# Gathering one chunk of every tenth or sixth group by single rows: the range of groups is widened

## The chip, the cores and the metric

The kernel runs on one core of one Trainium2 chip. The metric is the device time of one execution in microseconds; before the change it is 5949.51 us, the median of three runs (5947.85, 5949.51 and 5975.21 us). The profile is that of a separate execution.

## The reference

A graph layer in two rounds over 12,500 nodes of 128 features and 200,000 edges. The edges are sorted by their destination `dst`. Cut to what matters:

```python
h = jnp.maximum(_layernorm(x, axis=-1), 0.0)
# node_features = h
w = edge_weight / jnp.maximum(wsum, EPS)[dst]            # wsum, deg: sums over the edges of a node
feat = relu(h @ W_pool + b_pool)
msg = feat[src] * w[:, None]
neigh = segment_max(msg, dst, num_segments=N)            # layer 1
rst = h @ W1_self + neigh @ W1_neigh + b1
h1 = relu(rst / max(norm(rst), EPS))
msg2 = h1[src] * w[:, None]
neigh2 = segment_sum(msg2, dst, num_segments=N) / max(deg, 1)   # layer 2
out = relu(h1 @ W2_self + neigh2 @ W2_neigh + b2)
return x + out
```

What matters here are `feat[src]` and `h1[src]`: for each edge one row of 128 floats (512 bytes) is fetched from a table in device memory, at an address that only the data tell.

## The kernel before

**Tiling.** The edges go in groups of 512 (`G`), 391 of them (`NG`); the last, group 390, has 320 edges. A group has four chunks of 128 edges (group 390 has two whole chunks and one of 64). A chunk becomes a tile of 128 partitions (edges) by 128 floats.

**Stages.** A preparation normalizes the nodes, computes the table `feat_d` and stores it to device memory. It also builds the transposed edge tables (`srcT`, `ewT` and others). The first 14 groups (`FIRST`) are treated from `x` itself, so that they can be fetched before `feat_d` is done. Then comes layer 1, whose loop counter `i` is called a turn: turn `i` fetches group `i` and scales its rows (ACT, L868), transposes them (PE, L869), scans for the running maximum along the edges (DVE, L877) in turn `i + 1`, and selects and adds up the last edge of each node in the turns up to `i + 4`. Finished blocks of 128 nodes go through two matmuls and a norm (`nodes1`) and are stored to the second table, `h_d` (L758, L761). Layer 2 has the same 391 turns with less work in each: DVE builds a selection matrix (L965, L967), PE multiplies it with the fetched rows in turn `i + 1` (L985), DVE adds the result to a window (L994), and `nodes2` stores the output (L781). Layer 2 reads `h_d`, so its first gather waits until all of `h_d` is stored.

**Order.** The order of the instructions on each engine is written out by hand: what is emitted first in a turn stands first in its engine's queue. An engine runs its queue in order, so an instruction that waits holds up what is behind it. SP is the queue of most loads and stores: the weights' rows of the first groups (`gs`, L521), the two-group tiles that mark where a node begins (`kt`, L527), the stores of `h_d`, the index loads (`ri`, L672), and in layer 2 `xr` (L770) and `out` (L781).

**Two ways to fetch a chunk.** The usual one is an indirect DMA issued by GpSimd (POOL), one for each chunk (L446): it takes 128 indices from `srcT` and fetches 128 rows. The fetched groups stand in a ring of buffers. Up to group 63 the ring has 16 slots (some lent by tables that are not needed yet), later 8; a gather waits until its slot has been read.

The second way is the class `Rows`. In every tenth group of layer 1 (`every` 10) and every sixth of layer 2 (`every` 6), the first chunk is fetched by 128 single DMAs of 512 bytes, issued on the hardware queues of SP and ACT: 96 on SP in pieces of 16 and 32 on ACT in pieces of 4 in layer 1, 64 and 64 in pieces of 16 in layer 2. For such a group the 128 indices are loaded into one partition (`ri`, L672), DVE shifts them to byte offsets (L675), the issuing engine loads a piece's offsets into registers (L685) and issues its rows (L689) into the tile `ga`, of which there are three. The pieces are spread over the turns from `g - every - 1` on. The reader waits for all 128 rows (L703): ACT in layer 1, PE in layer 2. `takes` (L658) says which groups are fetched in this way: those that are divisible by `every` and lie between `first` and `end`. L836 and L951 make the two objects.

Of the kernel before, what the change touches and what calls it, by code (L numbers as in the profile page):

```python
# [39 lines left out]
def gnn_kernel(ctx, tc, x, src, dst, ew, w_pool, b_pool, w1s, w1n, b1, w2s, w2n, b2, out):  # L40
# [13 lines left out]
    nc = tc.nc  # L54
# [6 lines left out]
    NG = GF + 1  # L61
# [7 lines left out]
    feat_d = dram.tile([NP, D], F32, name="feat_d")  # L69
    h_d = dram.tile([NP, D], F32, name="h_d")  # L70
# [22 lines left out]
    wk = prep.enter_context(tc.tile_pool(name="n0", bufs=2))  # L93
# [23 lines left out]
    def buffer(g, wide):  # L117
        return ring[g % (WIDE if wide and g < LESS else RING)]
# [317 lines left out]
    def edges_of(g):  # L436

        ne = G if g < GF else TAIL
        return *divmod(g, P), ne, [(j, min(P, ne - j * P)) for j in range(-(-ne // P))]

    def gather(gt, table_d, g, byrow=None, only=None):
        t, r, ne, chunks = edges_of(g)
        for j, k in chunks if only is None else chunks[only:only + 1]:
            if j == 0 and byrow and byrow.takes(g):
                continue
            nc.gpsimd.indirect_dma_start(  # L446
                out=gt[:k, j, :], out_offset=None, in_=table_d[:, :],
                in_offset=bass.IndirectOffsetOnAxis(ap=srcT[:k, t, j, r:r + 1], axis=0))
        return gt
# [257 lines left out]
    def turns(behind):  # L707

        out = {}
        g = i = 0  # L710
        for n in range(HI):
            while g < NG - 1 and (g + 1 - LAG) * RHO < (n + 1) * P:
                g += 1
            i = max(i + 1, g + behind)
            out[i] = n
        return out
# [3 lines left out]
    def window_at(engine, g):  # L720

        if g % BL == 0:
            _, held[engine] = nc.values_load_multi_w_load_instructions(
                bases[0:1, g:min(g + BL, NG)], [engine], min_val=0, max_val=N - 1,
                skip_runtime_bounds_check_because="destinations of edges are nodes, as the gathers have it")
        return held[engine][g % BL]
# [11 lines left out]
    def linear_own(po, t, self_w):  # L738
        nc.tensor.matmul(po, hT[:, t, :], W[self_w], start=True, stop=False)  # L739
# [27 lines left out]
    def x_rows(wk, t, bufs):  # L767
        (q, p, view), = rows_of(x, t, 1)
        xr = wk.tile([P, D], F32, name="xr", bufs=bufs)
        nc.sync.dma_start(xr[:p, :], view[:, 0, :])  # L770
        return xr

    def nodes2(wk, ps, t, nT, xr):

        po = linear(ps, t, nT, "2s", "2n")
        yield
        (q, p, view), = rows_of(out, t, 1)
        o = wk.tile([P, D], F32)
        nc.vector.tensor_tensor(o[:p, :], po[:p, :], b2_all[:p, :], OP.add)
        nc.vector.scalar_tensor_tensor(o[:p, :], o[:p, :], 0.0, xr[:p, :], op0=OP.max, op1=OP.add)  # L780
        nc.sync.dma_start(view[:, 0, :], o[:p, :])  # L781

    def stages(steps):
        for _ in steps:
            pass


    with tc.manual_schedule(), tc.tile_pool(name="ew", bufs=3) as wk, \
# [44 lines left out]

        keep_rows(2, keep_tile())
        carry = NEG
        byrow = Rows(wk, feat_d, 10, [(nc.sync, 96, 16), (nc.scalar, 32, 4)], 30, NG - 16)  # L836
        for i in range(max(turn) + 6):
            if i >= NG:
                window_copy(i - 5)
# [107 lines left out]
    with tc.manual_schedule(), tc.tile_pool(name="ew2", bufs=3) as wk, \  # L947
            tc.tile_pool(name="ep2", bufs=3, space=PSUM) as ps:
        iota = ps.tile([P, LW], F32, bufs=1)
        nc.vector.tensor_copy(iota, cols[:, 0, :])  # L950
        byrow = Rows(wk, h_d, 6, [(nc.sync, 64, 16), (nc.scalar, 64, 16)], 6, NG - 4)  # L951
        nc.vector.memset(agg, 0.0)
        ss, pas, xrs = ({} for _ in range(3))
        turn = turns(3)
        late = None
        for i in range(max(turn) + 2):
            byrow.turn(i)
            byrow.rows(i, nc.sync)
            byrow.rows(i, nc.scalar)
            if i < NG:  # L960
                gts[i] = gather(buffer(i, False), h_d, i, byrow)
                t, r, ne, chunks = edges_of(i)
                ss[i] = wk.tile([P, Q, LW], F32, name="s")
                hit = ps.tile([P, Q, LW], F32, name="hit", bufs=1)
                nc.vector.tensor_tensor(hit, iota[:, None, :].to_broadcast([P, Q, LW]),  # L965
                                        locT[:, t, :, r:r + 1].to_broadcast([P, Q, LW]), OP.is_equal)
                nc.vector.tensor_tensor(ss[i], hit, w2T[:, t, :, r:r + 1].to_broadcast([P, Q, LW]),  # L967
                                        OP.mult)
            if i + 4 in turn:
                xrs[turn[i + 4]] = x_rows(wk, turn[i + 4], 6)  # L970
            if late is not None:
                stages(late)
                late = None
            if i in turn:
                n = turn[i]
                late = nodes2(wk, ps, n, agg[:, n * P:(n + 1) * P], xrs.pop(n))
                next(late)
            g = i - 1
            if 0 <= g < NG:
                chunks = edges_of(g)[3]  # L980
                pas[g] = ps.tile([P, LW], F32, name="pa")
                gt, s = gts.pop(g), ss.pop(g)
                for j, k in chunks:
                    rows_j = byrow.tile(g, nc.tensor) if j == 0 and byrow.takes(g) else gt[:k, j, :]
                    nc.tensor.matmul(pas[g], rows_j, s[:k, j, :], start=j == 0,  # L985
                                     stop=j == len(chunks) - 1)
            if i == NG - 1:
                for n in (HI - 2, HI - 1):
                    own[n] = ps.tile([P, D], F32, name="pn")
                    linear_own(own[n], n, "2s")  # L990
            g = i - 2
            if 0 <= g < NG:
                at = window_at(mybir.EngineType.DVE, g)
                nc.vector.tensor_tensor(agg[:, bass.ds(at, LW)], pas.pop(g), agg[:, bass.ds(at, LW)], OP.add)  # L994
        assert late is None
# [98 lines left out]
def build(inputs):  # L1094
    import numpy as np
    import concourse.bacc as bacc

    nc = bacc.Bacc("TRN2", target_bir_lowering=False, num_devices=1)
    arrays, args = {}, []
    for name in _INS:  # L1100
        a = np.ascontiguousarray(inputs[name])
        arrays[f"in_{name}"] = a
        args.append(nc.dram_tensor(f"in_{name}", a.shape, mybir.dt.from_np(a.dtype),
                                   kind="ExternalInput").ap())
    args.append(nc.dram_tensor("out", inputs["x"].shape, F32, kind="ExternalOutput").ap())
    with tile.TileContext(nc) as tc:
        gnn_kernel(tc, *args)
    return nc, arrays
# [7 lines left out]
```

## Time and profile before

| | |
|---|---|
| median of three runs | 5949.51 us |
| the profiled execution, its own time | 3844.75 us |
| span of the profile, first to last instruction | 3843.0 us |
| POOL busy | 2873.2 us (75%) |
| PE busy, granted clock 0.522 on average | 2317.6 us (60%) |
| DVE busy | 1712.7 us (45%) |
| ACT busy | 882.9 us (23%) |
| gathers from `feat_d` and from `h_d` (L446) | 1472 and 1499 |
| rows by single DMAs, layer 1: SP, ACT | 3360, 1120 |
| rows by single DMAs, layer 2: SP, ACT | 4096, 4096 |
| one row on SP or ACT (L689): issue, register move | 0.228 us, 0.029 us |
| one load of 16 registers on SP (L685) | 1.228 us |
| layer 1's last gather, layer 2's first gather, start | 1940.32 us, 1957.88 us |

The profiled execution is much shorter than the unprofiled runs, by 2104.8 us; nothing in the profile says where those have their additional time. All durations below come from the profiled execution.

The engines' names: PE is TensorE, DVE VectorE, ACT ScalarE, POOL GpSimd and SP SyncE; a name with a q (SPq, ACTq) is that engine's instruction queue, where DMAs are issued. In a line of the profile, `L446` is the line of the kernel, then come the engine, the operation, the tile written, the tiles read, and how often it occurs. "idle before" is the time for which the engine stood still ahead of it, with what ended that.

### The profile page before, as it was taken

To read this page: it belongs to the slowest core of one execution; us is meant where nothing else is said; L and a number is where in the kernel's file an instruction comes from. 1 tells how busy PE (TensorE), PEld (TensorE's weight loads), DVE (VectorE), ACT (ScalarE), POOL (GpSimd) and SP (SyncE) were. 2 spreads that over 40 slices of the span, in tenths; PEclk is the share of its full clock that TensorE was granted. 3 is DMA by queue.
4 is the path that set the end of the run, shared out by engine and by line. 5 is a ranking of instruction groups with operands and counts; after the bars stand their busy time and mean duration, and the time that the engine had idled before them with its cause. 6 is when DMAs were issued, how large, how long until landed. Compare 5 with 4: busy or idle time off the path is not lost.

```text
span 3843.0 us, 61269 instructions
## 1 busy us (share of the span) xinstructions
PE 2317.6 (60%) x8402; PEld 1790.5 (47%) x8402; DVE 1712.7 (45%) x4882; ACT 882.9 (23%) x2996; POOL 2873.2 (75%) x3061
## 2 busy tenths in 40 slices
PE   7666566666666666666655555555555555555555
PEld 5455454444444444444444444444444444444444
DVE  8877666666666666555542222222222222222221
ACT  7644444444444444444410000000000000000000
POOL 6777777777777777777767777777777777777776
PEclk9655555555555555555555555555555555555555
DMA  7433333323333333333312222222222222222222
GB/s 204 122 91 90 87 89 89 89 83 84 86 86 86 86 86 85 85 85 85 84 52 63 62 64 62 62 63 63 63 63 63 62 63 63 63 63 63 63 63 57
DMA packets 224215, 299.55 MB, mean 78 GB/s; under 512 B 70418, under 2 KB 147444, under 8 KB 223798
## 3 DMA queue, kind: packets, MB, share of 16 engines
q0 software_dynamic: 96864, 198.51, 19.8%
q1 hardware_dynamic: 115766, 93.43, 8.5%
q10 hardware_dynamic: 11168, 3.61, 0.6%
q14 instruction: 345, 2.83, 0.2%
q8 instruction: 72, 1.18, 0.1%
HBM read 275.50 MB, written 19.77 MB: 77 GB/s over the span
## 4 chain that ended last, share of the span: by engine, by line
DMA 55%; issue 11%; POOL 8%; PE 7%; DVE 6%; SPq 5%; ACT 4%; ACTq 3%; POOLq 0%; DVEq 0%
DMA gt<-h_d,srcT 33%; DMA gt<-feat_d,srcT 20%; POOL gt L446 8%; PE pa L985 3%; SPq L689 3%; ACTq L689 2%; ACT gs L868 2%; DVE pm L877 2%; PE pm L869 1%; SPq L685 1%; PE pn L739 1%; ACTq L685 1%; PE pn L735 1%; DVE sc L886 1%; DVE sel L897 1%
## 5 line engine op out<-in xcount | busy, mean ns | idle before, releaser
L446 POOL DMA_INDIRECT gt<-h_d,srcT x1499 | 1415.3, 944 | 474.1 <-issue 217.6
L446 POOL DMA_INDIRECT gt<-feat_d,srcT x1371 | 1295.2, 945 | 418.3 <-DMA gt<-feat_d,srcT 165.4
L985 PE MATMUL pa<-s,gt 128*128 128x48 f32 x2998 | 962.3, 425 | 809.2 <-DMA gt<-h_d,srcT 730.4
L985 PEld LDWEIGHTS pa<-s,gt 128*128 128x128 f32 x2998 | 749.7, 312 | 1024.3 <-DMA gt<-h_d,srcT 812.3
L869 PE MATMUL pm<-ident,gs 128*128 128x128 f32 x1507 | 573.0, 463 | 640.2 <-ACT gs L868 557.3
L877 DVE TENSOR_TENSOR_SCAN pm<-kt,carry,pm 128x512 f32<-128x512 bf16 x389 | 499.7, 1285 | 480.7 <-PE pm L869 473.7
L869 PEld LDWEIGHTS pm<-ident,gs 128*128 128x128 f32 x1507 | 284.0, 193 | 877.4 <-ACT gs L868 742.6
L994 DVE TENSOR_TENSOR agg<-pa,agg 128x48 f32 x391 | 81.2, 208 | 1351.6 <-PE pa L985 950.2
L868 ACT ACTIVATE gs<-gt,ewT 128x128 f32<-128x128 f32 x1371 | 489.6, 395 | 584.9 <-DMA gt<-feat_d,srcT 433.6
L926 PEld LDWEIGHTS pa<-sel,rows 128*128 128x128 f32 x1556 | 365.8, 324 | 51.7 <-ACT agg L819 51.3
L926 PE MATMUL pa<-sel,rows 128*128 128x48 f32 x1556 | 369.1, 385 | 17.1 <-ACT agg L819 16.4
L914 PE MATMUL pr<-ident,sc 128*128 128x128 f32 x782 | 243.7, 414 | 0.0
L897 DVE TENSOR_SCALAR sel<-cols,lastT,invT 128x48 f32<-128x48 f32 x782 | 211.0, 323 | 0.0
L886 DVE COPY_PREDICATED sc<-kt,pm 128x256 f32<-128x256 int16 x389 | 172.0, 442 | 13.2
L914 PEld LDWEIGHTS pr<-ident,sc 128*128 128x128 f32 x782 | 168.8, 225 | 0.1
L885 DVE COPY sc<-pm 128x256 f32<-128x256 f32 x391 | 162.0, 414 | 0.0
L967 DVE TENSOR_TENSOR s<-hit,w2T 128x192 f32<-128x192 f32 x391 | 139.8, 357 | 13.5
L904 ACT ACTIVATE rows<-pr 128x256 f32<-128x256 f32 x392 | 142.6, 364 | 0.5 <-PE pr L914 0.5
L965 DVE TENSOR_TENSOR hit<-iota,locT 128x192 f32<-128x192 f32 x391 | 140.4, 359 | 1.1
L819 ACT ACTIVATE agg<-pa 128x48 f32 x389 | 79.0, 203 | 180.5 <-PE pn L735 175.9
L675 DVE TENSOR_SCALAR ri<-ri 1x128 int32<-1x128 int32 x99 | 25.3, 256 | 196.9 <-DMA ri<-in_src 195.8
L739 PE MATMUL pn<-w_2s,hT 128*128 128x128 f32 x196 | 74.2, 483 | 0.0
(228 smaller groups left out, 1685.4 us busy)
## 6 DMA issues: line engine op xcount, KB each, us to landing
ga<-h_d SPq DMA_DIRECT2D x4096, 0.5 KB
ga<-h_d ACTq DMA_DIRECT2D x4096, 0.5 KB
ga<-feat_d SPq DMA_DIRECT2D x3360, 0.5 KB
kt<-keep_d SPq DMA_DIRECT2D x194, 256.0 KB
gt<-h_d,srcT POOLq DMA_INDIRECT x1499
gt<-feat_d,srcT POOLq DMA_INDIRECT x1371
ga<-feat_d ACTq DMA_DIRECT2D x1120, 0.5 KB
h_d<-h SPq DMA_DIRECT2D x98, 64.0 KB
```

The costliest lines, as they stand in the source:

```text
L446: nc.gpsimd.indirect_dma_start(out=gt[:k, j, :], out_offset=None, in_=table_d[:, :], in_offset=bass.IndirectOffsetOnAxis(ap=srcT[:k, t, j, ...
L689: row = eng.dma_start(ga[r + k:r + k + 1, :], self.bytes[None, bass.ds(at[k], 4 * D)])
L868: nc.scalar.activation(gs[:k, j, :], rows_j, AF.Copy, scale=ewT[:k, t, j, r:r + 1])
L869: nc.tensor.transpose(pms[i][:, j * P:j * P + k], gs[:k, j, :], ident[:k, :k])
L877: nc.vector.tensor_tensor_scan(pm[:, :ne], kt[:, :ne], pm[:, :ne], carry, op0=OP.add, op1=OP.max)
L885: nc.vector.tensor_copy(sc[:, :ne // 2], two[:, :, 1])
L886: nc.vector.copy_predicated(sc[:, :ne // 2], new[:, :, 1], two[:, :, 0])
L897: nc.vector.tensor_scalar(sels[g][:k, j, :], cols[:k, 1, :], lastT[:k, t, j, r:r + 1], invT[:k, t, j, r:r + 1], op0=OP.is_equal, op1=OP.mult)
L904: nc.scalar.activation(rws[g][:k, j, :], pr[:k, j, :], AF.Copy)
L914: nc.tensor.transpose(prs[g][:k, j, :], sc[:, j * P:j * P + k], ident)
L926: nc.tensor.matmul(pas[g], rows[:k, j, :], sel[:k, j, :], start=j == 0, stop=j == len(chunks) - 1)
L985: nc.tensor.matmul(pas[g], rows_j, s[:k, j, :], start=j == 0, stop=j == len(chunks) - 1)
```

## The change

Two numbers for each of the two `Rows` objects say where the row fetches begin and end. In layer 1 they began at group 30 and ended ahead of group 375 (`NG - 16`); now they begin at group 20 and end ahead of group 391 (`NG`). In layer 2 they ended ahead of group 387 (`NG - 4`); now they end ahead of group 391. Groups 20, 380 and 390 of layer 1 and group 390 of layer 2 are so fetched with three gathers (two in group 390) and 128 rows, where before it was one gather more and no rows.

```diff
-        byrow = Rows(wk, feat_d, 10, [(nc.sync, 96, 16), (nc.scalar, 32, 4)], 30, NG - 16)
+        byrow = Rows(wk, feat_d, 10, [(nc.sync, 96, 16), (nc.scalar, 32, 4)], 20, NG)
...
-        byrow = Rows(wk, h_d, 6, [(nc.sync, 64, 16), (nc.scalar, 64, 16)], 6, NG - 4)
+        byrow = Rows(wk, h_d, 6, [(nc.sync, 64, 16), (nc.scalar, 64, 16)], 6, NG)
```

The arguments are the pool, the table, `every`, the shares of the queues (queue, rows, rows in a piece), `first` and `end`. What `Rows` does with the last two, with the plan of the pieces:

```python
for g in range(first, end, every):
    begin = g - every - 1
    at = 0
    for eng, n, rb in share:
        for s in range(n // rb):
            turn = max(begin + s * every // (n // rb), 0)
            self.plan.setdefault(turn, []).append((g, eng, at, rb))
            at += rb
...
def takes(self, g):
    return g % self.every == 0 and self.first <= g < self.end
```

For group 20 of layer 1 the pieces on SP go out in turns 9, 10, 12, 14, 15 and 17, for group 390 in turns 379 to 387; for group 390 of layer 2 in turns 383, 384, 386 and 387.

## The prediction

> **What bounds the kernel now.** First the page's busy table with its costliest groups. GpSimd (POOL) is the busiest engine, and nearly all of that is one line, the indirect gather L446:
>
> ```profile
> PE 2317.6 (60%) x8402; PEld 1790.5 (47%) x8402; DVE 1712.7 (45%) x4882; ACT 882.9 (23%) x2996; POOL 2873.2 (75%) x3061
> ...
> L446 POOL DMA_INDIRECT gt<-h_d,srcT x1499 | 1415.3, 944 | 474.1 <-issue 217.6
> L446 POOL DMA_INDIRECT gt<-feat_d,srcT x1371 | 1295.2, 945 | 418.3 <-DMA gt<-feat_d,srcT 165.4
> ```
>
> 944 ns busy and, in the idle column, about 0.3 us before each. So the second view is POOL's list of waits (total us, times, longest us). If another engine held POOL up, a long wait would stand here:
>
> ```profile
> POOL gt L446 <- issue: 375.1, 1235, 0.5
> POOL gt L446 <- DMA gt<-feat_d,srcT: 165.4, 542, 0.3
> POOL gt L446 <- PE pa L985: 119.7, 392, 0.3
> ...
> POOL gt L446 <- DMA ri<-in_src: 16.6, 1, 16.6
> ```
>
> No wait of a gather is above 0.5 us but one, the passage from layer 1 to layer 2. The other releasers only name what finished last before a gap that is always there. The busy-by-stretch view gives the pace: 1321 instructions in 200-1850 us and 1458 in 1960-3780 us, so 1.249 and 1.248 us per gather. POOL's timeline at the passage (start, length, idle before):
>
> ```profile
> 1939.08 0.94 POOL L446 DMA_INDIRECT gt<-feat_d,srcT  x1 [0.30 <-issue]
> 1940.32 0.90 POOL L446 DMA_INDIRECT gt<-feat_d,srcT  x1 [0.30 <-issue]
> 1957.88 0.95 POOL L446 DMA_INDIRECT gt<-h_d,srcT  x1 [16.65 <-DMA ri<-in_src]
> ```
>
> The last gather of layer 1 feeds group 390; ACT takes it at 1942.67, the last nodes drain through PE, ACT and DVE, h is stored, and the next gather starts at 1957.88. The span is thus two rows of gathers at 1.249 us with a drain after each. The chain of waits agrees: it is 33% and 20% landing gathers, and 8% POOL.
>
> Third, SP's timeline, because the change gives SP work. Rows of layer 2:
>
> ```profile
> 3001.78 0.23 SPq L672 DMA_DIRECT2D ri<-in_src  x1
> 3003.41 5.11 SPq L689 DMA_DIRECT2D ga<-h_d  x16
> 3008.62 0.37 SPq L781 DMA_DIRECT2D out<-o  x1
> 3010.38 11.57 SPq L689 DMA_DIRECT2D ga<-h_d  x32
> 3022.01 0.36 SPq L770 DMA_DIRECT2D xr<-in_x  x1
> 3023.44 0.37 SPq L781 DMA_DIRECT2D out<-o  x1
> 3025.20 5.58 SPq L689 DMA_DIRECT2D ga<-h_d  x16
> 3030.89 0.23 SPq L672 DMA_DIRECT2D ri<-in_src  x1
> ```
>
> 16 rows take 5.1 us, and the register load before them (L685) 1.23 us: 6.4 us a piece. A layer 2 period (6 groups, 64 rows on SP) is 4 pieces, 25.6 us, plus about 1.6 us of other issues: 27.2 us, against 23 gathers x 1.249 = 28.7 us. A layer 1 period (10 groups, 96 rows) is 6 x 6.4 = 38.4 plus five kt, two or three h_d, one ri and gaps, about 43 us, against 39 x 1.249 = 48.7 us. SP has 5% to spare in layer 2 and 12% in layer 1. How near that is shows in DVE's waits of 200-800 us:
>
> ```profile
> DVE ri L675 <- DMA ri<-in_src: 94.5, 10, 11.2
> ```
>
> There ACT, PE and DVE still lag behind POOL, SP is their bound, and once in ten groups DVE stands 10 us or so for an index load that sits behind rows in SP's queue.
>
> **What the Trainium skill says.** "Perfetto Trace Analysis", section "DMA Instruction — SWDGE (GPSIMD)": the profiled end of a GpSimd DMA is when the last descriptor is made, not when the data has moved. So I price a gather by start-to-start spacing (1.249 us), not by its bar (0.944); the fixed 0.30 gap agrees. "DMA: Bandwidth & Descriptors", section "Issuing engines are not separate DMA queues": DMAs of all engines end on the same 16 DMA engines, and issuing elsewhere saves only the issuer's time. That is what the change trades; the page's queue table (19.8%, 8.5% and 0.6% busy) leaves the DMA engines room. "Runtime: NRT & Kernel Launch", section "The ~15µs preamble/postamble breakdown": profile total and reported time differ by about 6 us, profile longer. Here the profiled execution is 3844.75 us and the median 5949.51 us, 2104.8 us the other way, so that page doesn't explain it.
>
> **The change part by part.** Layer 1: row groups were 30, 40 to 370 (35); now 20 to 390 (38), adding 20, 380 and 390. Layer 2: 6 to 384 (64), now to 390 (65). Group 390 has 320 edges; its first 128 are a full chunk.
>
> Removed: one gather for each of four groups, 4 x 1.249 = 5.0 us of POOL. POOL never waits inside a layer, so all of it is on the path: 3.75 us before the 1957.88 gather, 1.25 us before the end.
>
> Added on SP: 3 x 96 + 64 = 352 rows x (0.228 issue + 0.029 register move) = 90 us, and 22 register loads x 1.228 = 27 us. On ACT: 3 x 32 + 64 = 160 rows, 41 us, with 24 loads x 0.489 and 4 long ones (up to 1.5), 18 us. Four ri loads (0.233) and four DVE shifts (0.217). All of it lies beside POOL's gathers, in periods where SP had only kt, h_d, xr and out. If that cover goes, an added period costs SP's excess over POOL's pace (the third rival).
>
> Moved in layer 1's tail: SP's kt loads and h_d stores of turns 369 to 387 stand behind row pieces, each up to 6.4 us later, as in the periods before. The last piece for 390 goes out in turn 387, three turns (15 us) before use; the final four h_d stores come later. At nothing. In layer 2's tail the last pieces go out in turns 383 to 387, four turns (20 us) before PE uses them; out stores wait for DVE anyhow. At nothing.
>
> Moved at the start: pieces in turns 9, 10, 12, 14, 15 and 17 stand before gs and kt loads. DVE's L889 of turns 9 and 10 ends at 150.0 and 155.6. A gs load is issued two turns (11 us) ahead of need, so 6.4 us behind a piece still fits. ACT's L851 runs at 148.33 with DVE needing it at 149.32: four rows there (1.5 us) can push DVE by up to 1 us in four turns. What hides it: POOL overwrites the slot of raw group 12 at 171.80 and its last reader, the product that L851 waits for at 164.69, ends just before, so 7 us. From 141 us SP needs 6 x 6.4 + 4 = 42 us, to 183; group 30's first piece went out at 184.82. So at most 2 us of lag is carried on, against slot margins of 13.4 us at group 72 (POOL 385.5, slot free 372.1) and 11.4 us at group 78. At nothing; lower bound 0, upper bound 3 us if the margins are half of what I read.
>
> Sum: 3844.75 - 5.0 = 3839.8, bounds -6 to 0. **To the median:** no view shows where the 2104.8 us are. If they are an offset, the gain stays 5.0 (5944.5); if everything is slower by 5949.51/3844.75 = 1.547, it is 7.7 (5941.8). I take the middle, 5943. The three runs of before spread over 27 us, 0.46%, so 0.5% is about what can be told from no change; my gain is 0.11%.
>
> **Rivals.** (1) Forecast: POOL is the bound, 5943. (2) The gathers go but the layer ends don't move: the drain at 1942-1957 is PE-paced, or the carried lag meets the slots at groups 72 to 80, and 3 to 5 us go back. For it: DVE's 11 us standings. Against: ACT takes each of the last gathers as it lands. 5949, at the worst 5955. (3) Slower: SP's row issue is the bound in unprofiled runs. The profile has it 5% and 12% away, and an SP slower by a factor f with POOL unchanged would lengthen all row periods: 35 x (43f - 48.7) + 64 x (27.2f - 28.7) = 2105 gives f = 1.74, which would explain the whole gap. Then each added layer 1 period costs 43 x 1.74 - 49.9 (40 gathers) = 25 us and the layer 2 one 27.2 x 1.74 - 30.0 = 17 us, 92 us together: 6041. It decides from f = 1.06 in layer 2 and 1.13 in layer 1. Against it: in the one execution seen POOL never waits for a row's consumer. (4) A gain over 0.5%: needs 30 us from four gathers, 7 us each; only spread between runs gives it, say 5915.
>
> **How the numbers follow.** Forecast 0.68, (2) 0.14, (3) 0.12, (4) 0.06. The first two lie within 0.5%: same 0.82, slower 0.12, faster 0.06. The range holds the first two with the spread of the runs, 5920 to 5968, and leaves 0.18 out.
>
> **What would show it.** In the changed kernel's profile: 1469 gathers of feat_d (1371 + 54 + 23 + 12 + 12 before, by buffer) and 1498 of h_d, pace still 1.249 us, no wait of POOL above 0.5 but the passage; the passage's gather near 1954.1, the span near 3838. Wrong if POOL shows waits of several us near 385 us (lag), if the passage's wait grows beyond 16.65 (drain or h_d late), or if the median moves by tens of us while the profiled span moves by 5: then rival (3).

## The result, and the profile after

| | before | after |
|---|---|---|
| median, on one chip | 5957.73 us (6 runs, 5947.85 to 5975.21) | 6011.47 us (6 runs, 5996.57 to 6031.12) |
| ratio, with its 95% interval | | 1.0085 [1.0069, 1.0101] |
| a profiled execution of it, span | 5930.5 us | 6005.4 us |
| gathers of `feat_d` and `h_d` in it | 1472, 1499 | 1469, 1498 |

The change makes the kernel slower by 0.85%, 51 us at before's median (41 to 60 by the interval). The profiled execution of before that the prediction reads (3844.75 us) is like none of the 87 timed executions of that kernel, the shortest of which took 5932.23 us, so its span isn't set against after's; the 5930.5 us are from a second profile of the unchanged kernel.

First the page of after: the busy table, the chain that ended last, and the gathers of `gt` (mean ns of one, then POOL's idle time before them and its main releaser).

```profile
PE 1991.3 (33%) x8402; PEld 1733.3 (29%) x8402; DVE 1683.3 (28%) x4886; ACT 851.6 (14%) x2996; POOL 2867.1 (48%) x3057
...
SPq L689 45%; SPq L685 6%; DVE pm L877 2%; SPq L527 1%; DMA ri<-in_src 1%; SPq L781 1%; DVE sel L897 1%; DVE sc L885 1%; DVE sc L886 1%; SPq L770 0%; SPq L761 0%; PE pf L550 0%; SPq L672 0%; PE pa L985 0%; SPq L150 0%
...
L446 POOL DMA_INDIRECT gt<-h_d,srcT x1498 | 1413.0, 943 | 1620.8 <-PE pa L985 970.3
L446 POOL DMA_INDIRECT gt<-feat_d,srcT x1368 | 1291.1, 944 | 1352.9 <-ACT gs L868 950.4
```

A gather is what it was, 0.943 us busy, but POOL is busy for only 48% of the span: the idle time before these gathers is 2973.7 us, where the first profile has 892.4, some 0.30 us before each. The chain of waits is no longer landing gathers: 45% is SP's row issue and 6% the register loads ahead of it. POOL's list of waits (total us, times, longest us) says for whom it stands:

```profile
POOL gt L446 <- PE pa L985: 970.3, 159, 17.6
POOL gt L446 <- ACT gs L868: 950.4, 175, 42.2
POOL gt L446 <- issue: 730.4, 2303, 2.1
...
POOL gt L446 <- DMA ri<-in_src: 51.5, 1, 51.5
```

In layer 2 it waits for PE and in layer 1 for ACT to read a slot of the ring, up to 17.6 and 42.2 us at a time. What holds these two up stands in the same list, under the other engines:

```profile
DVE ri L675 <- DMA ri<-in_src: 2204.4, 94, 33.7
...
PE pa L985 <- DVE s L967: 1809.9, 88, 47.7
...
DVE pm L877 <- DMA kt<-keep_d: 683.5, 84, 16.4
...
PE pa L985 <- PEq L703: 59.0, 15, 14.0
...
ACT gs L868 <- ACTq L703: 57.6, 16, 12.3
```

It is less the 128 rows themselves (L703) than what stands behind rows in SP's queue. DVE stands for the next index load `ri`, most of it in layer 2, and PE for the selection matrix `s`, which DVE builds only after that; in layer 1 DVE also stands for the `kt` loads, and ACT in turn for work of DVE and PE (266.2 us at L750, 332.6 at L819). In the first profile the three waits of DVE and PE were 195.8, 41.4 and 6.3 us.

SP's timeline in layer 2 of after, as in the prediction's third view (start, length, how many):

```profile
4618.66 0.23 SPq L672 DMA_DIRECT2D ri<-in_src  x1
4620.28 9.12 SPq L689 DMA_DIRECT2D ga<-h_d  x16
4630.11 0.70 SPq L781 DMA_DIRECT2D out<-o  x1
4632.95 22.59 SPq L689 DMA_DIRECT2D ga<-h_d  x32
4655.55 0.35 SPq L770 DMA_DIRECT2D xr<-in_x  x1
4656.00 0.46 SPq L781 DMA_DIRECT2D out<-o  x1
4657.86 5.16 SPq L689 DMA_DIRECT2D ga<-h_d  x16
4663.13 0.23 SPq L672 DMA_DIRECT2D ri<-in_src  x1
```

Between these lines lie register loads (L685), and the same 64 rows take 36.87 us (9.12 + 22.59 + 5.16), where the first profile had 22.26 (5.11 + 11.57 + 5.58). From one index load to the next it is 44.47 us, against 29.1 there. And 16 rows take 9.12 us in one place and 5.16 in another. POOL's timeline beside it (in brackets the idle time before) shows which is which:

```profile
4604.76 0.94 POOL L446 DMA_INDIRECT gt<-h_d,srcT  x1 [0.30 <-issue]
4622.29 0.94 POOL L446 DMA_INDIRECT gt<-h_d,srcT  x1 [16.59 <-PE pa L985]
4623.53 0.94 POOL L446 DMA_INDIRECT gt<-h_d,srcT  x1 [0.30 <-issue]
...
4653.62 0.94 POOL L446 DMA_INDIRECT gt<-h_d,srcT  x1 [0.30 <-issue]
4666.85 0.94 POOL L446 DMA_INDIRECT gt<-h_d,srcT  x1 [12.29 <-PE pa L985]
```

Rows that SP issues while POOL's gathers flow are slow (4623 to 4655); those issued while POOL stands (4657.86 to 4663.02) have the price of the first profile, 0.32 us each with the register move. It is so over the whole trace: from one row's register move to the next row's, SP's rows of layer 2 take 0.87 us on average where gathers start at most 1.3 us before and after, and 0.33 us where POOL has started none for 2.5 us. But gathers alone don't make rows slow: in the first profile all rows go beside gathers that are 1.249 us apart, at 0.33 us.

The stretch ends with the index load that SP issues at 4663.13:

```profile
4664.43 0.22 DVE L675 TENSOR_SCALAR ri<-ri 1x128 int32<-1x128 int32 x1 [26.92 <-DMA ri<-in_src]
4665.49 2.79 PE L985 MATMUL pa<-s,gt 128*128 128x48 f32 x12 [25.55 <-DVE s L967]
```

POOL goes on at 4666.85. So the two hold each other: gathers slow the rows, the loads behind late rows hold DVE, DVE holds PE, PE the slots, and POOL stops until the rows are out.

**Where the 51 us come in.** The next table follows two points through the traces: DVE's scan of a group (L877) in layer 1 and its addition (L994) in layer 2. Each number is how much later after is than the second profile of before, at the same group, in us:

```
layer 1   group  18   +9.4      layer 2   group   0  +53.3
          group  26  +10.5                group  40  +50.4
          group 190  +14.0                group 373  +66.5
          group 365  +26.5                group 375  +62.3
          group 390  +53.0                group 390  +76.7
```

About ten us come at the new rows of group 20, 26.5 between groups 365 and 390 of layer 1, 14.4 between 375 and 390 of layer 2. The rest accumulates over the middle, where the kernels are equal, and single executions differ by as much there.

At layer 1's end the passage shows it. POOL's timeline of after (the last gather of `feat_d` and the first of `h_d`), then SP's:

```profile
2930.08 0.90 POOL L446 DMA_INDIRECT gt<-feat_d,srcT  x1 [0.31 <-issue]
2982.52 0.95 POOL L446 DMA_INDIRECT gt<-h_d,srcT  x1 [51.53 <-DMA ri<-in_src]
```

```profile
2946.30 12.05 SPq L689 DMA_DIRECT2D ga<-feat_d  x32
2958.45 0.36 SPq L527 DMA_DIRECT2D kt<-keep_d  x1
2958.90 0.38 SPq L761 DMA_DIRECT2D h_d<-h  x1
2960.68 5.15 SPq L689 DMA_DIRECT2D ga<-feat_d  x16
2965.93 0.35 SPq L527 DMA_DIRECT2D kt<-keep_d  x1
2966.37 0.38 SPq L761 DMA_DIRECT2D h_d<-h  x1
```

POOL has fetched everything at 2931, and SP goes on issuing the rows of group 390 until 2965.83. Group 390 and the last stores of `h_d` wait for them, and layer 2 for those; the scan of group 390 starts at 2969.00, after the `kt` load that SP issues only at 2965.93. In before's second profile the passage's wait was 34.0 us.

### The profile page after: what moved, and what is told of

It reads as the page before. It is cut to its first block, busy times and chain, and to the rows that moved or that the text cites. A ratio compares the mean times of both kernels' runs of the same rounds, so it can differ in the third digit from the quotient of the medians.

```text
span 6005.4 us, 62358 instructions
## 1 busy us (share of the span) xinstructions
PE 1991.3 (33%) x8402; PEld 1733.3 (29%) x8402; DVE 1683.3 (28%) x4886; ACT 851.6 (14%) x2996; POOL 2867.1 (48%) x3057
## 3 DMA queue, kind: packets, MB, share of 16 engines
q0 software_dynamic: 96736, 198.24, 11.6%
## 4 chain that ended last, share of the span: by engine, by line
SPq 55%; issue 37%; DVE 5%; DMA 2%; PE 1%; ACT 0%; another core or an unknown queue 0%; ACTq 0%; DVEq 0%; PEldq 0%
SPq L689 45%; SPq L685 6%; DVE pm L877 2%; SPq L527 1%; DMA ri<-in_src 1%; SPq L781 1%; DVE sel L897 1%; DVE sc L885 1%; DVE sc L886 1%; SPq L770 0%; SPq L761 0%; PE pf L550 0%; SPq L672 0%; PE pa L985 0%; SPq L150 0%
## 5 line engine op out<-in xcount | busy, mean ns | idle before, releaser
L985 PE MATMUL pa<-s,gt 128*128 128x48 f32 x2996 | 681.6, 410 | 1841.7 <-DVE s L967 1809.9
L985 PEld LDWEIGHTS pa<-s,gt 128*128 128x128 f32 x2996 | 665.5, 332 | 1857.1 <-DVE s L967 1824.1
L869 PE MATMUL pm<-ident,gs 128*128 128x128 f32 x1507 | 459.9, 448 | 1105.7 <-DVE sc L886 432.3
L877 DVE TENSOR_TENSOR_SCAN pm<-kt,carry,pm 128x512 f32<-128x512 bf16 x389 | 497.7, 1279 | 912.1 <-DMA kt<-keep_d 683.5
L926 PE MATMUL pa<-sel,rows 128*128 128x48 f32 x1556 | 384.5, 396 | 605.8 <-ACT agg L819 368.6
L868 ACT ACTIVATE gs<-gt,ewT 128x128 f32<-128x128 f32 x1368 | 436.0, 390 | 229.2 <-issue 227.5
L994 DVE TENSOR_TENSOR agg<-pa,agg 128x48 f32 x391 | 79.9, 204 | 834.1 <-remote 387.2
L819 ACT ACTIVATE agg<-pa 128x48 f32 x389 | 79.6, 205 | 889.5 <-remote 432.7
L985 PE MATMUL pa<-s,ga 128*128 128x48 f32 x130 | 41.1, 416 | 271.1 <-issue 183.1
```

The source lines that it names most:

```text
L868: nc.scalar.activation(gs[:k, j, :], rows_j, AF.Copy, scale=ewT[:k, t, j, r:r + 1])
L869: nc.tensor.transpose(pms[i][:, j * P:j * P + k], gs[:k, j, :], ident[:k, :k])
L877: nc.vector.tensor_tensor_scan(pm[:, :ne], kt[:, :ne], pm[:, :ne], carry, op0=OP.add, op1=OP.max)
L926: nc.tensor.matmul(pas[g], rows[:k, j, :], sel[:k, j, :], start=j == 0, stop=j == len(chunks) - 1)
```

## The experiments

Each kernel is compared with before on its own chip. Layer 2's end alone, half of the rows, the moved share and the rows without gathers ran on a chip where before took 6038.03 us, both ends and the quarter on one with 5955.46, the others on one with 5956.58; between chips the ratios are compared, and traces only with care.

### Before, once more

No edit.

> The kernel before, run once more, for a trace of the kind of execution that is timed. Row theory (SP's issue of single rows bounds the timed executions): about 5955 us, SP's pieces of 16 rows much above the 5.1 us of the first profile, and POOL with waits of tens of us behind PE and ACT. Gather theory (POOL's gathers are the bound, only dearer when timed): about 5955 us, gathers 1.9 to 2.0 us apart and no long waits of POOL.

5947.27 us, 0.9989 [0.9972, 1.0006], span 5930.5 us. POOL's waits:

```profile
POOL gt L446 <- PE pa L985: 955.9, 152, 17.9
POOL gt L446 <- ACT gs L868: 936.8, 177, 39.9
...
POOL gt L446 <- DMA ri<-in_src: 34.0, 1, 34.0
```

From one row to the next SP takes 0.65 us on average in layer 1 and 0.61 in layer 2, against 0.33 in the first profile. So before is in the same regime as after, and every timed execution of it took as long. The third line is again the passage between the layers.

### No rows at all

```diff
-... 30, NG - 16)
+... NG, NG)
-... 6, NG - 4)
+... NG, NG)
```

> No group is fetched by rows in either layer: 99 gathers more (35 + 64), 12672 row DMAs fewer. Row theory: POOL becomes the bound at 1.249 us a gather, 3844.75 + 99 x 1.249 = 3968 us, at any rate under 4300. Gather theory: 99 x 1.9 = 190 us more, about 6140 us.

4653.56 us, 0.781 [0.7796, 0.7823]: 99 more gathers than before (124 us of POOL at 1.249) and 12,672 fewer single rows, and 1303 us less. The direction is that of the theory that the rows are the burden; the size fell short of it, for POOL isn't the bound even then:

```profile
POOL gt L446 <- issue: 656.8, 2117, 2.2
POOL gt L446 <- ACT gs L868: 410.6, 186, 25.1
POOL gt L446 <- remote: 244.3, 223, 4.3
POOL gt L446 <- PE pa L985: 138.9, 202, 3.0
```

The waits for PE are down from 955.9 to 138.9 us, those for ACT from 936.8 to 410.6. Here POOL also waits for releasers that the trace doesn't name ("remote"), and so do other engines: DVE's longest waits in total, 1496.7 us at L994 and 914.0 at L877, are for such.

### The three parts of the change, each alone

The start alone:

```diff
-... 30, NG - 16)
+... 20, NG - 16)
```

> The start alone: layer 1's rows from group 20, ends as before. Row theory: one more period of ten turns at SP's pace (73.5 us in the trace of the changed kernel against 50 us for 40 gathers), up to 24 us more, about 15 because DVE bounds the first 14 turns anyhow. Gather theory: 1 to 2 us less.

5959.55 us, 1.0008 [0.9995, 1.0021]: not told from nothing by the times. Its trace has the same step as after's, 8.6 us later at group 18 and 13.0 at group 26. But of the kernels below that keep before's start, one is 1.8 us earlier at group 26 and one 6.7 later, so a step of this size isn't told from the spread of executions either.

Layer 1's end alone:

```diff
-... 30, NG - 16)
+... 30, NG)
```

> Layer 1's end alone: rows up to group 390, start and layer 2 as before. Row theory: two more periods, up to 47 us more, about 30 because rows stop in turn 387. Gather theory: 2.5 to 4 us less.

5979.87 us, 1.0038 [1.0013, 1.0062], 23 us. In its trace 26.6 us appear between groups 365 and 390 (from +13.1 to +39.7), as in after.

Layer 2's end alone:

```diff
-... 6, NG - 4)
+... 6, NG)
```

> Layer 2's end alone: rows up to group 390 of layer 2, layer 1 as before. Row theory (SP's issue bounds; turns without rows run faster, turns with rows at SP's pace): 10 to 18 us more, the step that the trace of the changed kernel has over that of before in layer 2's last 20 turns. Gather theory: 1 to 2 us less.

6047.05 us, 1.0012 [1.0001, 1.0022], 7 us at that chip's 6038.03: a little under what was expected of it. In its trace 15.7 us appear between groups 375 and 390 (from +108.6 to +124.3).

### Both ends together

```diff
-... 30, NG - 16)
+... 30, NG)
-... 6, NG - 4)
+... 6, NG)
```

> Both ends widened, the start as before (30, NG and 6, NG). If each added period costs by itself: layer 1's end has shown +0.38% and layer 2's end +0.12%, together 1.0050 or about +30 us, and what is left to the whole change (1.0085) is the start. If the parts are not additive (layer 1's lag is carried into layer 2, or the passage between the layers hides one of them): 1.002 or below, or 1.008 and above, with the start at nothing.

5987.0 us, 1.0061 [1.0039, 1.0083]. The parts' 0.38% and 0.12% are within that interval, and 0.61% with the start's 0.08% is 0.69%, the lower edge of after's. So the parts add up as far as the intervals tell, and most of the loss is at the ends. What is left to the start is 0.08% by its own run and 0.24% by the difference of after and both ends.

### Half of the rows, and a quarter

```diff
-Rows(wk, feat_d, 10, ... 30, NG - 16)
+Rows(wk, feat_d, 20, ... 40, NG - 16)
-Rows(wk, h_d, 6, ... 6, NG - 4)
+Rows(wk, h_d, 12, ... 12, NG - 4)
```

> Half the row groups (every 20th group of layer 1, every 12th of layer 2), the others gathered. Theory of SP as one bound among others: with half the rows SP needs about 73 us in 20 turns that POOL needs 99 us for, so it falls out and the time is that without rows, 4600 to 4750 us. Theory of a price for each row, wherever the bound is (1304 us for 12672 rows, 0.103 us each): half way, about 5300 us.

4837.56 us, 0.8013 [0.7993, 0.8032], which is 4773 us at 5957 and a little above the range expected of SP as one bound among others. Taking half of the rows away brings 0.199 of before's time, taking all away 0.219. So there is no price per row: nine tenths of the cost come with the second half of the rows, when SP's issue is late. The rows haven't become quicker (SP takes 1.01 us from one to the next on average), but DVE's waits for `ri` fall, from 583.7 us in before's second profile to 20.7 in layer 1 and from 1729.8 to 590.5 in layer 2. Against the kernel without rows (ratios 0.8013 and 0.781) half the rows are still no gain, though 49 gathers are gone.

A quarter (every 40th group from 80, every 24th from 24):

> Rows in every 40th group of layer 1 (from 80) and every 24th of layer 2 (from 24): a quarter of the rows, about 25 gathers removed. If below the threshold rows are free and a removed gather is worth 1.249 us: about 31 us under the 4653.6 us of the kernel without rows, 4620. If rows beside gathers always cost something: half the rows cost 184 us over none, so a quarter some 90 us over none, 4745.

4678.0 us, 0.7861 [0.7841, 0.7882]. Neither expectation was met: no gain from the gathers that are gone, and a cost of about 30 us (0.0051 of 5955), a third of what was expected of rows that always cost. The two kernels ran on different chips, so the cost is less sure than that there is no gain. No kernel here is faster than the one without rows.

### A third of SP's rows of layer 1 to ACT

```diff
-[(nc.sync, 96, 16), (nc.scalar, 32, 4)], 30, NG - 16)
+[(nc.sync, 64, 16), (nc.scalar, 64, 4)], 30, NG - 16)
```

> Layer 1's rows shared 64 to 64 between SP and ACT in place of 96 to 32; the same rows and groups. Theory of SP's queue as the bound: SP's part of a layer 1 period falls by about a third, from 74 to some 52 us, so 35 periods save some 700 us, about 5250 us. Theory of a price for each row on whichever queue: no change, 5957 us; if ACT's issue stands before its own scaling work, some more.

5628.66 us, 0.9318 [0.9296, 0.934], 409 us less with the same number of rows and gathers. A price per row would have given nothing; SP's queue as the bound was to give 700. Some 180 of these were never there: without any rows a period still takes 59.0 us, 14.7 less than before's, and 35 times that is about 515. What is missing beyond that may be ACT's, which isn't shown; its list of waits now has

```profile
ACT gs L868 <- issue: 840.9, 218, 8.7
```

where before had 221.3 us in 162 waits (longest 4.9): ACT's own rows now stand ahead of its scaling. DVE's waits for `ri` in layer 1 are down to 5.0 us. A period of ten groups in layer 1 takes 63.8 us, against 75.2 in the kernel with layer 2's end widened, which ran on the same chip with before's layer 1; layer 2, untouched, takes 46.6 us, against 46.8 there.

### The rows of layer 2 without its gathers

```diff
-                gts[i] = gather(buffer(i, False), h_d, i, byrow)
+                gts[i] = buffer(i, False)
```

The kernel leaves out all gathers of layer 2, so PE multiplies with what is in the ring's buffers; the single rows remain.

> Layer 2 leaves out its gathers: the three or four gathered chunks of a group are whatever the buffers still hold, the rows go on as before. Theory that SP's row issue is slowed by the gathers beside it: SP's pieces of 16 rows take 5.1 us, a layer 2 period 27 us, layer 2 about 1800 us in place of 3000, the whole about 4750 us. Theory that SP's issue is slow by itself when timed: pieces as long as in the kernel before, layer 2 stays at 3000 us, 5950 us.

4806.26 us, 0.7957 [0.7933, 0.798]. SP's timeline in layer 2:

```profile
3618.75 0.23 SPq L672 DMA_DIRECT2D ri<-in_src  x1
3620.37 5.57 SPq L689 DMA_DIRECT2D ga<-h_d  x16
3626.04 0.38 SPq L781 DMA_DIRECT2D out<-o  x1
3627.85 11.57 SPq L689 DMA_DIRECT2D ga<-h_d  x32
3639.47 0.36 SPq L770 DMA_DIRECT2D xr<-in_x  x1
3639.93 0.39 SPq L781 DMA_DIRECT2D out<-o  x1
3641.66 5.14 SPq L689 DMA_DIRECT2D ga<-h_d  x16
3646.91 0.23 SPq L672 DMA_DIRECT2D ri<-in_src  x1
```

The same 64 rows take 22.28 us, and the period is 28.16: the prices of the first profile, from a kernel whose layer 1 kept its gathers and its period of 75.2 us. In this kind of execution it is the gathers beside them that make SP's rows slow; why the first profile's gathers did not, this run doesn't tell. Nor was it tried to take only `ri` and `kt` out of SP's queue, with rows and gathers as they were, so how much of the loss goes through these loads isn't measured.

## Why the prediction was wrong

Predicted were 5943 us, in a range of 5920 to 5968; it became 6011.47. Its terms can be measured in the steady middle of the layers, as the mean time of ten groups in layer 1 (scans of groups 40 to 365) and of six in layer 2 (additions of groups 40 to 370). The ring has fewer slots at group 365 than at group 40, which brings the scan nearer to its gathers; that is how a mean can be 1.1 us below POOL's pace. The first profile's chip isn't on record; before's second profile and the kernel without rows ran on one chip, half of the rows and the last line on another, where before is 1.4% slower.

| us | layer 1, ten groups | layer 2, six groups |
|---|---|---|
| gathers at 1.249, as predicted | 48.7 | 28.7 |
| first profile of before | 47.6 | 28.7 |
| before, second profile | 73.7 | 46.0 |
| after | 74.3 | 46.2 |
| without rows | 59.0 | 34.0 |
| half of the rows | 60.7 | 35.6 |
| layer 2 without its gathers | 75.2 | 28.1 |

- **The step that failed** is "POOL never waits inside a layer, so all of it is on the path". That was so in one execution that no timed one resembles. The prediction saw that 2104.8 us were unexplained, offered "an offset" or "everything is slower" by one factor, and took the middle of the two. It was neither: the usual spacing of two gathers is 1.249 us in all these traces, and the time is lost in waits between them. Those above 0.5 us sum to 17.2 us in the first profile and to 2131.5 us in before's second, 2114 more, and the second span is 2088 us longer.
- **The cost of the added rows**, "all of it lies beside POOL's gathers", failed with it. SP had no 5% and 12% to spare; it had less than nothing. A layer 2 period was priced right for an SP left alone (27.2 worked out, 28.1 measured without gathers; layer 1 wasn't run so). Beside gathers the periods are 1.71 times the 43 us (73.7) and 1.69 times the 27.2 (46.0). The prediction had read the way the lag travels, DVE standing for an index load behind rows in SP's queue, but put the loads that it moved at nothing.
- **The removed gathers** were counted right (1469 and 1498) and their pace too, but a gather saved only lengthens the next wait where POOL waits so much. The kernels with half and a quarter of the rows show no gain from the gathers that they save either.
- **Layer 1's tail** at nothing: 26.5 us, with SP's rows ending 35 us after POOL's last gather. **Layer 2's tail** at nothing: 14.4 us. **The start**, at most 3 us: about 10 in the trace, 5 by the times with nothing inside the interval; it stays open whether it cost anything. At the two tails the cover named was POOL's gathers at 1.249 us, and it wasn't there.
- **The third rival**, SP's row issue as the bound with a factor of 1.74, is what happened, with the sign and nearly the factor of the runs (1.71 and 1.69); that gathers slow the rows was not in it. It had 12 chances in 100, because the one execution seen spoke against it. Its size was too large, 92 us against 51. The term that was off is what a period costs *without* rows: it took POOL's pace, 49.9 and 30.0 us, where the kernel without rows takes 59.0 and 34.0. With these an added period costs 73.7 - 59.0 = 14.7 us in layer 1 and 46.0 - 34.0 = 12.0 in layer 2, and three and one of them 56 us, inside the measured 41 to 60, though the one period of the start, alone, showed only -3 to 13 us. The same two prices over before's 35 and 64 periods give 1283 us, and the span without rows is 1282 us shorter than before's (5930.5 - 4648.2): both come from the same two traces, and say that the loss is spread evenly over the periods.

The Trainium skill's "DMA: Bandwidth & Descriptors", section "Issuing engines are not separate DMA queues", says that issuing on several engines saves the sequencer's time only, usually little beside the DMA. Here that time was the bound: 64 rows of 512 bytes held SP's sequencer for 36.87 us in after, while over after's span the packets of the software queue, which has the gathers, took 11.6% of the 16 DMA engines' time, and those of the largest hardware queue 5.4%.

Open: what the kernel without rows waits for, which is 9 us a period in layer 1 and 4 us in layer 2 above POOL's pace, with a wait of 34.6 us at the passage where the first profile has 16.65; and why one execution ran without the slowing. It wasn't met again.

## What to carry to other kernels

Before pricing an edit from a profile, set the profiled time beside the timed ones: where they are a factor apart, ask of each queue how far the profile has it from being the bound (here SP, 5% and 12%), and weigh that rival by the unexplained gap and not by the profile alone. A second way to fetch that relieves a busy engine is worth its gathers only as long as its own queue has slack beside the first. Ask what else stands in that queue, and who waits for it: here it was an index load. Take the second way out altogether once and time that before widening it. The price of one more period is the difference between periods with and without it under the timed conditions, not against the ideal pace of the engine relieved.

## What the runs showed of the hardware

That indirect gathers by GpSimd can slow single DMAs issued on another engine's hardware queue was not expected: SP's rows of layer 2 took 0.87 us beside flowing gathers and 0.33 us while POOL stood (after), and 0.33 us without layer 2's gathers. They don't always: in the first profile rows took 0.33 us beside gathers at the same pace. Nor do the bytes alone account for it, for there the DMA engines moved 63 GB/s in the middle of layer 2, and in before's second profile 39.

The slow stretches go in steps of about 0.70 us. In before's second profile 2457 of SP's records, register moves among them, are followed by the next at 0.66 to 0.76 us, in the first profile 8; without layer 2's gathers it is 959 in layer 1 and 3 in layer 2. ACT has the steps too, 1063 against 38 in the first profile, nearly all in layer 2, where its pieces have 16 rows. Its pieces of four rows in layer 1 take 0.39 us a row beside gathers and 0.40 while POOL stands. What makes the steps no trace shows. Since half of them follow a row's register move, it may be the supply of instructions as well as the issue of DMAs; that wasn't tested.
